# Graph layer and mixture of experts on one core: four more adds by GpSimd, column blocks loaded in halves, the first expert slot run tile by tile

## The chip, the cores and the metric

The kernel runs on one core of a Trainium2 chip. Its time is the device time in microseconds; where several executions are shown, the median counts, and lower is better.

## The reference

There are 2048 nodes with 256 features, 67,584 edges sorted by destination, and 8 experts of which each node takes the best two. Cut to what matters:

```python
    edge_index = jnp.stack([src, dst])
    x = x + _L0_gnn_ref(_layernorm(x, axis=-1), edge_weight, edge_index, node_vec1)
    x = x + _L0_ffn_ref(_layernorm(x, axis=-1)[None], L0_ffn_Wr, ...)[0]

def _L0_gnn_ref(x, values, indices, bias):
    gathered = values[:, None] * x[indices[1]]
    return jax.ops.segment_sum(gathered, indices[0], num_segments=2048) + bias

def _L0_ffn_ref(x, Wr, br, ln_g, ln_b, W1, b1, W2, b2):
    probs = jax.nn.softmax(xt @ Wr + br, axis=-1)
    top_p, top_idx = jax.lax.top_k(probs, 2)
    weights = top_p / top_p.sum(axis=-1, keepdims=True)
    xe = xn[None] * ln_g[:, None] + ln_b[:, None]
    h = jax.nn.gelu(jnp.einsum('end,edh->enh', xe, W1) + b1[:, None], approximate=False)
    y = jnp.einsum('enh,ehd->end', h, W2) + b2[:, None]
    # the two chosen experts' rows, weighted and summed
```

`xn` is the layer norm of `xt` once more. Hidden width is 1024.

## The kernel before

**First half: the graph layer.** The sum over edges is made into a matrix product. The 2048 columns (destinations) are cut into 16 *column blocks* `cb` of 128. For each block the kernel builds the dense block of the adjacency matrix (2048 rows by 128 columns) and multiplies it with the normalised features. The build runs in 32 steps `n`, two per block (`h = n % 2`). In a step:

- VectorE makes, for step n + 1, the one-hot operands `hl` (line 328), `eq` (335) and `hr` (343). Both `hl` and `hr` have two buffers.
- TensorE multiplies them for step n in 96 small matmuls (`make_cols`, line 367) into `pa` (three PSUM buffers), and ScalarE copies `pa` to `ar` (line 370; pool `rowsp`, three buffers).
- SP stores `ar` to a DRAM tile `ad` (line 371), which turns the layout around: step h = 0 writes rows 0 to 63 of the block, step h = 1 rows 64 to 127. After the second store SP loads the whole block back as `ac` (line 374), 1 MB. SP issues its transfers in program order, so the load stands in the queue until both stores have landed, and whatever is behind it stands too.
- `ac` tiles come from two pools: `cols_0` with three buffers (blocks 0 to 2, then 8 to 10) and `cols_1` with five (blocks 3 to 7, then 11 to 15). A buffer is free when the last product that reads it is done.

Column blocks are consumed in five groups (0-2, 3-6, 7-10, 11-13, 14-15). From n = 8 on each step also runs one *visit* (`dense`, line 383): the product of one group with two of the 16 row blocks, into a PSUM tile of two buffers. A group has eight visits: group 0 at n = 8 to 15, group 1 at n = 16 to 23, group 2 at n = 24 to 31, the rest after the loop. The result of a visit is added to `acc` one step later. For group 0 (`add_apart`) ScalarE copies it to SBUF tiles `st` (five buffers), adding the bias `node_vec1`, and GpSimd starts a transfer that adds `st` to `acc` (line 396). For later groups VectorE adds from PSUM (`add`, line 388).

The order on every engine here is the order of the program (`manual_schedule`). GpSimd also issues, in between, the gathers of edge windows (line 242) and runs (line 223). At n = 12 SP issues two fills of zeros (lines 588, 590).

**Second half: the experts.** After the graph layer the nodes are normalised, routed, and listed by expert. The work is cut into *slots*: 256 rows (two tiles of 128) that go to one expert. For a slot the rows are gathered by GpSimd, turned by TensorE and scaled by VectorE (`turn_rows`, lines 1027, 1030, `scale_rows`, line 1042), multiplied with W1 followed by GELU on ScalarE (`layer_1`, lines 1068, 1070), multiplied with W2 (`layer_2`, line 1082), weighted by VectorE (line 1085) and scattered with addition to DRAM (line 1090). The first three slots (`early`) are filled from the first ten row blocks alone, so that TensorE has expert work while the rest of the routing runs. In the first of them, `whole[0]`, six warming matmuls precede the turning, and two pieces of routing on TensorE (`list_batch_0` at c = 4, `sum_counts` at c = 7) are placed between the eight column tiles c of `layer_1`.

Of the kernel before, what the change touches and what calls it, by code (L numbers as in the profile page):

```python
# [10 lines left out]
F32 = mybir.dt.float32  # L11
# [3 lines left out]
AF = mybir.ActivationFunctionType  # L15
OP = mybir.AluOpType
# [6 lines left out]
P = 128  # L23
# [4 lines left out]
def kernel(  # L28
# [30 lines left out]
    nc = tc.nc  # L59
    N, D = x.shape  # L60
    NE, _, H = W1.shape
    E = src.shape[0]
    NB = N // P
    EJ = E // P
    KD = D // P
    KH = H // P
# [19 lines left out]
    NU = NF + NE  # L86
    DX = D + NE
    RW = D + 4
    AHEAD = 2
    EARLY = 3  # L90

# [261 lines left out]
    def make_cols(n, hl, hr):  # L353


        cb, h = n // 2, n % 2
        if h == 0:
            ads[cb] = dram.tile([P, NB, P], F32, name="ad", bufs=CB)
        ad_v = ads[cb].rearrange("(m j) b r -> (j b) m r", m=GB // QP)
        ar = rowsp.tile([P, GH // QP, P], F32, name="ar")  # L360
        for m0 in range(0, GH // QP, 4):
            pa = ps_a.tile([P, 4, P], F32, name="pa")
            for m in range(4):
                for i in range(3):
                    for j in range(QP):
                        g = (m0 + m) * QP + j
                        nc.tensor.matmul(pa[j * RK:(j + 1) * RK, m, :], hr[:, g, i, :],  # L367
                                         hl[:, g, :], start=(i == 0), stop=(i == 2),
                                         tile_position=(0, j * RK))
            nc.scalar.copy(ar[:, m0:m0 + 4, :], pa)  # L370
        nc.sync.dma_start(ad_v[:, h * GH // QP:(h + 1) * GH // QP, :], ar)
        if h == 1:
            acs[cb] = (cols_0 if cb in GROUPS[0] or 8 <= cb < 11 else cols_1).tile([P, NB, P], F32, name="ac")
            nc.sync.dma_start(acs[cb], ads[cb])

    def dense(blocks, b, between={}):

# [9 lines left out]
    def add(b, pa):  # L387
        nc.vector.tensor_add(acc[:, b:b + 2, :], acc[:, b:b + 2, :], pa[:, :, :DX])  # L388

    def add_apart(b, pa):  # L390
        st = stage.tile([P, 2, DX], F32, name="st")
        for i in range(2):
            nc.scalar.activation(st[:, i, :D], pa[:, i, :D], AF.Identity,
                                 bias=nv_c[:, b + i:b + i + 1], scale=1.0)
        nc.scalar.copy(st[:, :, D:], pa[:, :, D:DX])
        nc.gpsimd.dma_start(acc[:, b:b + 2, :], st, accum_op=OP.add)

    ads, acs = {}, {}
# [2 lines left out]
    with tc.manual_schedule(engines=ALL):  # L401
# [111 lines left out]
        for n in range(NH):  # L513
# [30 lines left out]
                b = {7: 0, 10: 4, 12: 8, 14: 12}[n]  # L544
                weigh_n(slice(b, b + 4))
            for p in late:
                (add_apart if n <= NB else add)(*p)
            late = []
            make_cols(n, *hots.pop(n))
            g, k = divmod(n - NB // 2, NB // 2)  # L550
# [161 lines left out]
    with tc.manual_schedule(engines=ALL - {ET.Pool}):  # L712
# [74 lines left out]
        def count(s):  # L787

            sel = s["sel"]
            more = route.tile([P, NE], F32, name=f"more{s['i']}", bufs=1)  # L790
            nc.vector.tensor_reduce(more, sel.rearrange("p b e -> p e b"), AX.X, OP.add)
            nc.vector.tensor_add(seen, seen, more)

        def sum_counts(s):

            sel, seen_b = s["sel"], s["seen"]
            s["pc"] = pc = counts[:, s["i"], :s["n"], :]
            nc.tensor.matmul(pc, before, sel, start=True, stop=False)
# [222 lines left out]
        def turn_rows(s, warm=0):  # L1021


            xs = sets[s.set][0]
            pt = ps_x.tile([P, KD, TS], F32, name="px")
            for i in range(warm):
                nc.tensor.matmul(pt[:, 0, :P], ident, ident, start=True, stop=True)
            for t in range(s.n):
                for k in range(KD):
                    nc.tensor.transpose(pt[:, k, t * P:(t + 1) * P],  # L1030
                                        xs[:, t, k * P:(k + 1) * P], ident)
            scale_rows(s, pt)
# [26 lines left out]
        def layer_1(s, between={}):  # L1059
            xs, w1, w2, ec, b2r = sets[s.set]  # L1060
            xeT = heads[s.head][0]
            hT = slotp.tile([P, KH, TS], F32, name="hT")
            for c in range(KH):
                if c in between:
                    between[c]()
                ph = ps_h.tile([P, TS], F32, name="ph")[:, :s.n * P]
                for k in range(KD):
                    nc.tensor.matmul(ph, w1[:, k, c * P:(c + 1) * P], xeT[:, k, :],  # L1068
                                     start=(k == 0), stop=(k == KD - 1))
                nc.scalar.activation(hT[:, c, :s.n * P], ph, AF.Gelu, bias=ec[:, c:c + 1],  # L1070
                                     scale=1.0)
            return hT

        def layer_2(s, hT, put, between={}):
            w2 = sets[s.set][2]
            xeT, wt, b2w = heads[s.head]
            for t in range(s.n):
                if t in between:
                    between[t]()
                py = ps_y.tile([P, D], F32, name="py")  # L1080
                for c in range(KH):
                    nc.tensor.matmul(py, hT[:, c, t * P:(t + 1) * P], w2[:, c, :],  # L1082
                                     start=(c == 0), stop=(c == KH - 1))
                ys = slotp.tile([P, D], F32, name="ys", bufs=4)
                nc.vector.scalar_tensor_tensor(ys, py, wt[:, t:t + 1], b2w[:, t, :], op0=OP.mult,  # L1085
                                               op1=OP.add)
                put(s, t, ys)
# [87 lines left out]
        ps_h = ctx.enter_context(tc.tile_pool(name="ps_h", bufs=3, space=PSUM))  # L1175
        ps_y = ctx.enter_context(tc.tile_pool(name="ps_y", bufs=2, space=PSUM))
        roots(last_b)
        turn_rows(whole[0], 6)
        enlist_rows(first_b)
        count(first_b)  # L1180
        take_seen(last_b)

# [7 lines left out]
        best(last_b, 0)  # L1190
        best(last_b, 1)
        select(last_b)
        hT = layer_1(whole[0], {4: list_batch_0, 7: lambda: sum_counts(last_b)})
        scale_recs(last_b, range(NB - NA))
        shares(last_b)
        nc.scalar.activation(warm, eps_sb, AF.Gelu)
# [91 lines left out]
```

## Time and profile before

| what | value |
|---|---|
| median of three runs | 491.8 us (488.56 to 492.25) |
| the profiled execution | 487.33 us |
| its span, first to last instruction | 485.6 us |
| mean granted TensorE clock | 0.989 |
| busy: TensorE, VectorE, ScalarE, GpSimd | 441.7, 268.2, 198.4, 173.3 us |
| loop over n ends on TensorE | about 189.4 us |
| first slot's layer 1 begins on TensorE | 231.43 us |

A row of the profile names the source line, the engine, the operation, and the tiles as out<-in. In a timeline a row begins with its start and its duration in us; what stands in square brackets is the idle time of the engine before it and what ended that. PE is TensorE, DVE VectorE, ACT ScalarE, POOL GpSimd, and SP the engine that issues most transfers; SPq rows are the issuing itself. An fp32 matmul shows as two records, so a product of four column blocks with two row blocks is x16.

### The profile page before, as it was taken

To read this page: it belongs to the slowest core of one execution; us is meant where nothing else is said; L and a number is where in the kernel's file an instruction comes from. 1 tells how busy PE (TensorE), PEld (TensorE's weight loads), DVE (VectorE), ACT (ScalarE), POOL (GpSimd) and SP (SyncE) were. 2 spreads that over 40 slices of the span, in tenths; PEclk is the share of its full clock that TensorE was granted. 3 is DMA by queue.
4 is the path that set the end of the run, shared out by engine and by line. 5 is a ranking of instruction groups with operands and counts; after the bars stand their busy time and mean duration, and the time that the engine had idled before them with its cause. 6 is when DMAs were issued, how large, how long until landed. Compare 5 with 4: busy or idle time off the path is not lost. (4 is left out here: it accounts for less than half of the span.)

```text
span 485.6 us, 12168 instructions
## 1 busy us (share of the span) xinstructions
PE 441.7 (91%) x5008; PEld 378.2 (78%) x5008; DVE 268.2 (55%) x556; ACT 198.4 (41%) x488; POOL 173.3 (36%) x141
## 2 busy tenths in 40 slices
PE   1587798889998999998999999999999999999995
PEld 0466677677886888887888888888888888879784
DVE  5999999999999974247772312334323212210011
ACT  2567669652423220066572233332334332224320
POOL 5560737654130000013724333564343444222123
PEclk9988899999999999999999999999999999999999
DMA  3777769988778776995438987799999676542341
GB/s 96 236 206 225 235 185 259 268 208 235 222 203 247 225 214 187 343 374 163 98 98 266 332 262 220 225 349 369 349 330 292 175 228 190 167 115 26 79 154 43
DMA packets 88372, 105.58 MB, mean 217 GB/s; under 512 B 9920, under 2 KB 77616, under 8 KB 86192
## 3 DMA queue, kind: packets, MB, share of 16 engines
q1 hardware_dynamic: 79072, 88.95, 57.7%
q0 software_dynamic: 9200, 15.67, 14.4%
q8 instruction: 44, 0.72, 0.6%
q14 instruction: 24, 0.20, 0.1%
q10 hardware_dynamic: 32, 0.04, 0.0%
HBM read 75.11 MB, written 29.47 MB: 215 GB/s over the span
## 5 line engine op out<-in xcount | busy, mean ns | idle before, releaser
L1068 PE MATMUL ph<-xeT,w 128*128 128x256 f32 (+1 forms) x576 | 122.7, 369 | 3.6 <-PEq L1242 1.2
L1082 PE MATMUL py<-w,hT 128*128 128x256 f32 x544 | 120.4, 379 | 0.0
L1070 ACT ACTIVATE hT<-ph,ec 128x256 f32<-128x256 f32 (+1 forms) x144 | 65.7, 460 | 128.8 <-PE ph L1068 74.2
L1068 PEld LDWEIGHTS ph<-xeT,w 128*128 128x128 f32 x576 | 103.7, 190 | 18.2 <-issue 2.9
L1082 PEld LDWEIGHTS py<-w,hT 128*128 128x128 f32 x544 | 102.2, 190 | 13.2
L1090 POOL DMA_INDIRECT y_d<-ys,to_i x30 | 48.0, 1598 | 115.0 <-DVE ys L1085 75.5
L383 PE MATMUL py<-xn_lo,ac 128*128 128x264 f32 x352 | 85.3, 394 | 4.1 <-DMA ac<-ad 3.6
L383 PEld LDWEIGHTS py<-xn_lo,ac 128*128 128x128 f32 x352 | 64.8, 190 | 17.2 <-DMA ac<-ad 4.5
L328 DVE TENSOR_TENSOR hl<-k,iota_b 128x4096 bf16<-128x4096 bf16 (+1 forms) x33 | 73.2, 2219 | 1.2 <-ACT k L289 1.0
L367 PE MATMUL pa<-hl,hr 128*32 128x128 bf16 x3072 | 54.9, 231 | 15.3 <-DVE hr L343 9.0
L367 PEld LDWEIGHTS <-hr 128*32 128x32 bf16 x3072 | 48.0, 103 | 25.3 <-issue 11.6
L1085 DVE SCALAR_TENSOR_TENSOR ys<-py,wt,b2w 128x256 f32<-128x256 f32 x34 | 16.3, 483 | 80.4 <-PE py L1082 77.2
L343 DVE TENSOR_TENSOR hr<-eq,w 128x3072 bf16<-128x3072 bf16 x32 | 56.2, 1758 | 1.9 <-DVE eq L335 0.5
L1042 DVE TENSOR_SCALAR xeT<-px,ec 128x256 f32<-128x256 f32 (+1 forms) x38 | 18.4, 525 | 67.0 <-PE px L1030 67.0
L370 ACT COPY ar<-pa 128x512 f32<-128x512 f32 x64 | 35.4, 592 | 39.0 <-PE pa L367 23.5
L995 POOL DMA_INDIRECT xs<-xr_d,to_i x32 | 33.5, 1045 | 15.0 <-DVE ys L1085 5.5
L242 POOL DMA_INDIRECT win_s<-in_src,at_i x8 | 15.9, 1987 | 60.7 <-DVE at_i L238 46.2
L383 PE MATMUL py<-xn_hi,ac 128*128 128x264 f32 x160 | 36.5, 388 | 0.3 <-PEq L613 0.3
L383 PEld LDWEIGHTS py<-xn_hi,ac 128*128 128x128 f32 x160 | 30.2, 190 | 5.7 <-PEq L613 0.7
L388 DVE TENSOR_TENSOR acc<-acc,py 128x528 f32<-128x528 f32 x29 | 20.3, 700 | 19.6 <-PE py L383 19.5
L1057 ACT ACTIVATE b2w<-b,wt 128x256 f32<-128x256 f32 x36 | 16.3, 499 | 25.7 <-DVE wt L1055 22.6
L335 DVE TENSOR_TENSOR eq<-k,iota_b 128x1024 bf16<-128x1024 bf16 x32 | 21.9, 683 | 0.0
(218 smaller groups left out, 331.5 us busy)
## 6 DMA issues: line engine op xcount, KB each, us to landing
w<-in_L_ffn_W SPq DMA_DIRECT2D x40, 1024.0 KB, 9.7
ad<-ar SPq DMA_DIRECT2D x32, 512.0 KB, 7.5
ac<-ad SPq DMA_DIRECT2D x16, 1024.0 KB, 6.0
b<-in_L_ffn_b SPq DMA_DIRECT2D x20, 128.0 KB, 8.6
acc<-st POOLq DMA_DIRECT2D x8, 264.0 KB
acc<-in_x SPq DMA_DIRECT2D x4, 512.0 KB, 4.5
out<-y_d SPq DMA_DIRECT2D x4, 512.0 KB, 5.0
xr_d<-rec SPq DMA_DIRECT2D x1, 1300.0 KB
```

The costliest lines, as they stand in the source:

```text
L328: nc.vector.tensor_tensor(hl.rearrange("p g (n t) -> p g n t", t=2)[:, m], two(k2[:, 0], g, P)[:, m], pair(P)[:, m], OP.is_equal)
L335: nc.vector.tensor_tensor(eq.rearrange("p g (n t) -> p g n t", t=2), two(k2[:, 1], g, RK), pair(RK), OP.is_equal)
L343: nc.vector.tensor_tensor(hr.rearrange("p g i (n t) -> p (g i) n t", t=2), eq[:, :, None, :].to_broadcast([P, GH, 3, RK]), w[:, :, None, : ...
L367: nc.tensor.matmul(pa[j * RK:(j + 1) * RK, m, :], hr[:, g, i, :], hl[:, g, :], start=(i == 0), stop=(i == 2), tile_position=(0, j * RK))
L370: nc.scalar.copy(ar[:, m0:m0 + 4, :], pa)
L383: nc.tensor.matmul(pa[:, i, :DX], acs[c][:, b + i, :], xn(c), start=(c == blocks[0]), stop=(c == blocks[-1]))
L388: nc.vector.tensor_add(acc[:, b:b + 2, :], acc[:, b:b + 2, :], pa[:, :, :DX])
L995: nc.gpsimd.indirect_dma_start(out=(sets[s.set][0] if into is None else into)[:, t, cols], out_offset=None, in_=(xr_d if rows is None else ...
L1068: nc.tensor.matmul(ph, w1[:, k, c * P:(c + 1) * P], xeT[:, k, :], start=(k == 0), stop=(k == KD - 1))
L1070: nc.scalar.activation(hT[:, c, :s.n * P], ph, AF.Gelu, bias=ec[:, c:c + 1], scale=1.0)
L1082: nc.tensor.matmul(py, hT[:, c, t * P:(t + 1) * P], w2[:, c, :], start=(c == 0), stop=(c == KH - 1))
L1090: st = nc.gpsimd.indirect_dma_start(out=y_d[:, :], out_offset=bass.IndirectOffsetOnAxis(ap=tos[s.to][:, t:t + 1], axis=0), in_=ys, in_offs ...
```

## The change

Three edits are made together.

1. For the second group, the visits whose results are added at n = 17 to 20 also go through `st` and GpSimd's adding transfer; the copy to `st` is then one plain ScalarE copy without bias. The other four visits stay with VectorE.
2. The load of a column block is split into two halves of 64 partitions. Half 0 reads only rows that the first store wrote. In step h = 1 it is issued ahead of the second store, except for blocks 11 and 15, where it follows that store. Half 1 always comes last.
3. In the first slot, turning, scaling and layer 1 go one tile of 128 rows at a time. The second tile is turned inside the first tile's layer (ahead of c = 4); column tiles go in pairs that share a PSUM tile; the two pieces of routing move to the second tile's layer, at c = 2 and c = 6.

```diff
+    WAIT = 11, 15
...
+        def get_half(i):
+            rows = slice(i * P // 2, (i + 1) * P // 2)
+            nc.sync.dma_start(acs[cb][rows], ads[cb][rows])
+
+        if h == 1:
+            acs[cb] = (cols_0 if cb in GROUPS[0] or 8 <= cb < 11 else cols_1).tile([P, NB, P], F32, name="ac")
+            if cb not in WAIT:
+                get_half(0)
         nc.sync.dma_start(ad_v[:, h * GH // QP:(h + 1) * GH // QP, :], ar)
         if h == 1:
-            acs[cb] = (cols_0 if cb in GROUPS[0] or 8 <= cb < 11 else cols_1).tile([P, NB, P], F32, name="ac")
-            nc.sync.dma_start(acs[cb], ads[cb])
+            if cb in WAIT:
+                get_half(0)
+            get_half(1)
...
-    def add_apart(b, pa):
+    def add_apart(b, pa, first):
         st = stage.tile([P, 2, DX], F32, name="st")
-        for i in range(2):
-            nc.scalar.activation(st[:, i, :D], pa[:, i, :D], AF.Identity,
-                                 bias=nv_c[:, b + i:b + i + 1], scale=1.0)
-        nc.scalar.copy(st[:, :, D:], pa[:, :, D:DX])
+        if first:
+            for i in range(2):
+                nc.scalar.activation(st[:, i, :D], pa[:, i, :D], AF.Identity,
+                                     bias=nv_c[:, b + i:b + i + 1], scale=1.0)
+            nc.scalar.copy(st[:, :, D:], pa[:, :, D:DX])
+        else:
+            nc.scalar.copy(st, pa[:, :, :DX])
         nc.gpsimd.dma_start(acc[:, b:b + 2, :], st, accum_op=OP.add)
...
-                (add_apart if n <= NB else add)(*p)
+                if n <= NB + 4:
+                    add_apart(*p, n <= NB)
+                else:
+                    add(*p)
...
+        def turn_tile(s, pt, t, warm=0):
...
+            rows = slice(t * P, (t + 1) * P)
+            for i in range(warm):
+                nc.tensor.matmul(pt[:, 0, :P], ident, ident, start=True, stop=True)
+            for k in range(KD):
+                nc.tensor.transpose(pt[:, k, rows], xs[:, t, k * P:(k + 1) * P], ident)
+            for k in range(KD):
+                nc.vector.tensor_scalar(xeT[:, k, rows], pt[:, k, rows], ec[:, KH + k:KH + k + 1],
+                                        ec[:, KH + KD + k:KH + KD + k + 1],
+                                        op0=OP.mult, op1=OP.add)
+
+        def layer_1_tile(s, hT, t, between={}):
...
+            for c in range(0, KH, 2):
+                if c in between:
+                    between[c]()
+                ph = ps_h.tile([P, TS], F32, name="ph").rearrange("p (i r) -> p i r", r=P)
+                for i in range(2):
+                    for k in range(KD):
+                        nc.tensor.matmul(ph[:, i, :], w1[:, k, (c + i) * P:(c + i + 1) * P],
+                                         xeT[:, k, rows], start=(k == 0), stop=(k == KD - 1))
+                for i in range(2):
+                    nc.scalar.activation(hT[:, c + i, rows], ph[:, i, :], AF.Gelu,
+                                         bias=ec[:, c + i:c + i + 1], scale=1.0)
...
-        turn_rows(whole[0], 6)
+        pt = ps_x.tile([P, KD, TS], F32, name="px")
+        hT = slotp.tile([P, KH, TS], F32, name="hT")
+        turn_tile(whole[0], pt, 0, 6)
         enlist_rows(first_b)
+        layer_1_tile(whole[0], hT, 0, {4: lambda: turn_tile(whole[0], pt, 1)})
...
-        hT = layer_1(whole[0], {4: list_batch_0, 7: lambda: sum_counts(last_b)})
+        layer_1_tile(whole[0], hT, 1, {2: list_batch_0, 6: lambda: sum_counts(last_b)})
```

More of the change, by code (lines that the diff above doesn't have):

```diff
@@ L1072, in layer_1 @@
             return hT
+        def turn_tile(s, pt, t, warm=0):
+            xs, w1, w2, ec, b2r = sets[s.set]
+            xeT = heads[s.head][0]
+            rows = slice(t * P, (t + 1) * P)
[8 more added lines that the diff above has]
+        def layer_1_tile(s, hT, t, between={}):
+            xs, w1, w2, ec, b2r = sets[s.set]
+            xeT = heads[s.head][0]
+            rows = slice(t * P, (t + 1) * P)
+            for c in range(0, KH, 2):
[9 more added lines that the diff above has]
+                                         bias=ec[:, c + i:c + i + 1], scale=1.0)
         def layer_2(s, hT, put, between={}):
```

## The prediction

> **What bounds the kernel now.** I read the page first. TensorE is busy for 91% of the span, and the chain that ended last covers only the last 15 us, so the question is where TensorE waits, and for whom. I then read TensorE's timeline. From 231.43 us to the end it has almost no gap, and from 189.4 to 228 it has almost none either. Time that it wins or loses earlier reaches the end one for one. These are its waits in the second half of the loop over n:
>
> ```profile
> 100.65 1.60 PE L383 MATMUL py<-xn_lo,ac 128*128 128x264 f32 x6
> 103.89 2.49 PE L383 MATMUL py<-xn_lo,ac 128*128 128x264 f32 x10 [1.64 <-DMA ac<-ad]
> ...
> 113.72 0.85 PE L367 MATMUL pa<-hl,hr 128*32 128x128 bf16 x48 [1.01 <-ACT ar L370]
> ...
> 149.68 2.49 PE L383 MATMUL py<-xn_lo,ac 128*128 128x264 f32 x10 [1.98 <-DMA ac<-ad]
> ...
> 157.64 1.52 PE L367 MATMUL pa<-hl,hr 128*32 128x128 bf16 x96
> ...
> 162.85 1.52 PE L367 MATMUL pa<-hl,hr 128*32 128x128 bf16 x96
> ```
>
> Lines two and four are the first visits of the second and third group (n = 16 and 24), stopped at their last column block (6 and 10) until its load lands. Line three waits for a copy into `ar`, which waited for a store `ad<-ar`. The last two give a step without waits: 5.21 us, about 0.6 more where keys are turned, so about 10.7 per column block of two steps. VectorE is busy almost throughout but is not what TensorE waits for. Its `hr` for n = 24 starts at 141.11, takes 1.76 and is ready at 142.87; TensorE begins that step at 144.64. From n = 17 to 30 VectorE is 1.8 to 4.4 us ahead.
>
> Behind all three waits stands SP's queue. The list of what SP waits for, then its timeline:
>
> ```profile
> SPq L374 <- DMA ad<-ar: 103.9, 16, 13.6
> ...
> SPq L371 <- ACT ar L370: 40.7, 14, 11.2
> ```
> ```profile
> 84.05 0.33 SPq L374 DMA_DIRECT2D ac<-ad  x1
> ...
> 98.47 0.33 SPq L374 DMA_DIRECT2D ac<-ad  x1
> 98.85 2.24 SPq L371 DMA_DIRECT2D ad<-ar  x2
> 114.73 0.33 SPq L374 DMA_DIRECT2D ac<-ad  x1
> 115.11 1.82 SPq L371 DMA_DIRECT2D ad<-ar  x2
> 124.35 0.33 SPq L374 DMA_DIRECT2D ac<-ad  x1
> 124.73 1.12 SPq L371 DMA_DIRECT2D ad<-ar  x2
> 133.35 0.33 SPq L374 DMA_DIRECT2D ac<-ad  x1
> ```
>
> The reader is to see the rhythm. SP stands at each load for the landing of the block's stores, and when it is released the next block's two stores are already waiting and leave at once. So here SP and the transfers set the pace. From load to load undisturbed it takes 9.0 to 9.6 us, less than TensorE's 10.7. From 72.49 to 114.73, however, it takes 11.6, 14.4 and 16.3, and in that stretch the first group's eight transfers by GpSimd run:
>
> ```profile
> 99.18 3.69 POOL L396 DMA_DIRECT2D acc<-st  x4
> ```
>
> 42.2 us instead of three times 9.3 leaves 14.3 us for eight such transfers, two zero fills and gathers. Four transfers (1.06 MB) were in one interval of 16.3, which is 7.0 over; they are about three quarters of GpSimd's bytes there, so I charge about **1.3 us each**.
>
> **The change, part by part.**
>
> *Adds by GpSimd.* VectorE loses four `acc<-acc,py` at n = 17 to 20, 4 x 0.70 = 2.8 us. TensorE lags VectorE there, so this is worth 0 unless TensorE's waits go away. ScalarE gains four copies of 128x528 (the nearest row, 128x512, takes 0.59): 2.4 us in a stretch where it is busy a third of the time, 0. They stand ahead of the `ar` copies and need only the visit that TensorE has just ended. GpSimd issues four more transfers, queued behind the three window gathers of n = 17 (until 114.8); the next gathers come at 131.7, so nothing waits on its queue. What they cost is transfer time: 4 x 1.3 = **5.2 us** just where SP is the pace. Low bound 0 (they fall where the transfer engines idle, as while SP waits), high bound 4 x 1.75 = 7.0 (all of the excess above).
>
> *Half loads.* The count of bytes stays. What changes is the order on SP: half 0 now stands ahead of the second store and waits there for the landing of the first store. Behind it on SP are that store, and with three `ar` buffers ScalarE's copy three steps on, then TensorE's `pa`. One round per block (wait for two stores, load) becomes two (wait for one store, half load). Cost of a round: this answer is the time from issue to landing of a whole load (source line 374).
>
> ```profile
> DMA to landing us min/median/max: 5.9/6.0/6.1
> ```
>
> A load and two stores behind it take 9.0 to 9.3 from load to load, so a store behind a load adds 1.5 to 1.65. A store alone, issued at 25.14, releases the load at 28.88: 3.7, so about 1.4 to 2.2 is latency and the load's own transfer is 3.8 to 4.6. A new round is latency 1.4 to 2.2, half a load 2.3 to 1.9, a store 1.5: **5.2 to 5.6 us**, two to a block 10.4 to 11.2. I take 10.6, nearest to the low end because the longer latency is seen once, on an idle queue. That is **1.3 us more per block** than 9.3, and all the spare time that SP has against TensorE's 10.7. On the other side the last wait gets shorter: half 1 lands 1.9 to 2.3 us sooner after its issue than a whole load.
>
> Here the Trainium skill (DMA: Bandwidth & Descriptors, "Rules for kernel authors") speaks against the change: transfers on disjoint partition halves share the same engines, so one over all partitions is advised. Its fit (same page, "Anatomy of one DMA", given for GpSimd's path) is 2.0 us plus bytes over 436 GB/s. By it a new round with 1 MB is 4.4 us, 8.8 a block, and would hide under TensorE's 10.7; the measured 9.0 for 2 MB (6.8 by the fit) says that its rate is too high here, so I keep 10.6.
>
> Sum to block 6. SP still has idle time early on (the 40.7 us of waits for `ar`). Walking the first stores with 5.3 a round, half 1 of block 3 leaves at about 65.3, where the load now leaves at 62.61: 2.7 late. Three further blocks at 1.3 make 3.9; half 1 lands 2.2 sooner. Together +4.4, so TensorE's wait at n = 16 grows from 1.64 to about 6. Sum to block 10: four more blocks, 5.2, and the added transfers, 5.2, of which TensorE's own delay of 4.4 covers part. So does the time that SP now waits for `ar` from 114.7 on (three blocks of 9.6 instead of 9.0, 1.8). 5.2 + 5.2 - 4.4 - 1.8 = 4.2, and 0.4 for short waits on `ar` before: 4.6. VectorE's 2.8 us stay hidden, as TensorE lags more. After n = 24, blocks 11 and 15 keep the old order and the loop ends with SP again close behind. The loop thus ends about **9.0 us later**.
>
> *First slot tile by tile.* The start of this slot now, and the pace of a 128-column layer in the later half slots:
>
> ```profile
> 228.68 0.38 PE L1030 MATMUL px<-ident,xs 128*128 128x128 f32 x2
> 230.35 0.44 PE L1030 MATMUL px<-ident,xs 128*128 128x128 f32 x2 [1.29 <-DMA xs<-x_d,to_i]
> 231.43 3.74 PE L1068 MATMUL ph<-xeT,w 128*128 128x256 f32 x16 [0.64 <-DVE xeT L1042]
> ```
> ```profile
> 444.37 3.73 PE L1068 MATMUL ph<-xeT,w 128*128 128x128 f32 x32
> ```
>
> Tile 0's rows are there at 228.68. Two transposes (0.38) and two scalings of 128 columns (0.41 each, overlapping: about 0.8) let the layer begin at about 229.95 instead of 231.43: 1.5 won. 64 matmuls of half width take 2 x 3.73 = 7.46 against 7.07 (0.4 lost); tile 1's transposes now stand inside (0.4 lost). Tile 1's rows land before they are wanted (230.3 against 231.8), and VectorE has its chain of `select` ready at about 237.4 as now, just before the counts at 238. ScalarE needs 3.44 for eight half-width GELUs, under TensorE's 3.73. Net **-0.7 us** (+0.5 if the counts wait for VectorE, -1.5 at best).
>
> Sum: +9.0 - 0.7 = +8.3. The profiled execution took 487.33 (span 485.6) and would take 495.6; the median shown is 491.8, 4.5 above it, so I add the same: **500 us**.
>
> **Rivals.** *SP gets slower but TensorE does not see it* (chance 0.25): a round nearer 5.0 and the added transfers filling idle stretches, so the halves' later issue and sooner landing cancel. For it: the transfer share is only 0.80 between 115 and 190. Against: SP already paces at 115. Change between -5 and +5; with waits as now, 491.8 - 0.7 = 491.
> *The waits vanish* (0.14): half 1 lands early enough at n = 16 and 24 and `ar` never waits; 1.64 + 1.01 + 1.98 = 4.6, with 0.7: 486.5. It decides where a round stays under about 4.7 us, so that SP reaches block 6 no later than now and half 1's 2 us come out as gain; then VectorE's 2.8 us would be needed, since its lead falls to 1.8. This is the other side.
> *A whole-block wait* (0.04): if the second store had to wait for half 0's landing (2 to 4 us more, fourteen blocks), 30 us and more, beyond 520. That now both stores of a block leave within 1.1 us (124.73) speaks against such coarse tracking.
>
> **How the numbers follow.** The slower queue has 0.57: from +5 (transfers at their low bound, rounds 5.2) to +19 (all high). Slower by over 1% (4.9 us, about what a measurement of this kernel can tell from no change) takes this and the whole-block wait: 0.61. Within 1%: 0.25. Faster: 0.14. The likeliest case alone is 497 to 511. The range runs from 486, which takes in the second rival and the near half of the third, to 511, leaving out the top of the likeliest and the whole-block wait.
>
> **What would show it.** Right: from block 3 on SP standing at half 0 with the second store issued right after; issues of half 1 10 us and more apart and late at blocks 6 and 10; TensorE waiting for `ac` 5 us or so at n = 16 and more than 2 at n = 24. Wrong: waits for `ac` below 1 us and the loop ending before 189. For the slot: its first `ph` 1.3 us after the first transposes, with no wait between tiles. A store that lands in 3 us behind a half load would overturn the round, and with it the sign.

## The result and the profile after

The changed kernel takes **522.2 us** (median of 7 runs, 518.42 to 530.54) where the kernel before takes 491.8 (median of 7, 488.56 to 494.44): +30.4 us between the medians. Some executions of every kernel fall into a slower state; ratios are of the others alone, here 1.0597, interval 1.0547 to 1.0646. The forecast was 500 with a range to 511. The direction was right, the size was not.

The profiled execution took 530.54 us (span 528.5), 8.4 above its median, at a mean granted clock of 0.942, while that of before lay 4.5 below its median; so only 30 of the 43 us between the two profiles stand in the medians. The waits for column blocks and for the first rows that follow come back, about as long, in two further profiles of the changed kernel (e0 and e12); the wait for `ar` does not (0.48 and 0.18 us there).

First the same views as before. Rows from the list of groups: busy us and mean ns of one, then the idle time ahead of the group and what ended most of it. The first fence is of before, the second of after.

```profile
L383 PE MATMUL py<-xn_lo,ac 128*128 128x264 f32 x352 | 85.3, 394 | 4.1 <-DMA ac<-ad 3.6
...
L367 PE MATMUL pa<-hl,hr 128*32 128x128 bf16 x3072 | 54.9, 231 | 15.3 <-DVE hr L343 9.0
```
```profile
L393 PE MATMUL py<-xn_lo,ac 128*128 128x264 f32 x352 | 91.9, 415 | 24.0 <-DMA ac<-ad 24.0
...
L368 PE MATMUL pa<-hl,hr 128*32 128x128 bf16 x3072 | 58.7, 239 | 16.0 <-DVE hr L344 9.5
```

For the dense products both figures have grown: 20 us more waiting for column blocks, and 6.6 us more for the same matmuls. TensorE's timeline says where; the first fence is again of before (its other rows stand in the prediction):

```profile
189.43 15.29 PE L383 MATMUL py<-xn_hi,ac 128*128 128x264 f32 x68
```
```profile
65.53 3.86 PE L393 MATMUL py<-xn_lo,ac 128*128 128x264 f32 x8 [3.22 <-DMA ac<-ad]
...
110.85 0.85 PE L368 MATMUL pa<-hl,hr 128*32 128x128 bf16 x48 [2.66 <-ACT ar L371]
...
126.96 4.74 PE L393 MATMUL py<-xn_lo,ac 128*128 128x264 f32 x10 [13.72 <-DMA ac<-ad]
...
180.62 4.25 PE L393 MATMUL py<-xn_lo,ac 128*128 128x264 f32 x10 [7.04 <-DMA ac<-ad]
...
221.63 15.29 PE L393 MATMUL py<-xn_hi,ac 128*128 128x264 f32 x68
...
269.78 0.69 PE L1099 MATMUL px<-ident,xs 128*128 128x128 f32 x2 [8.74 <-DMA xs<-x_d,to_i]
```

In the second fence, rows one, three and four are the first visits of the three groups, at n = 8, 16 and 24, each stopped at its last block (2, 6, 10). Row two is a wait for a copy into `ar`. Then come the end of the loop, 221.63 where it was 189.43 (+32.2); and the first slot, whose rows are now late (they were there at 228.68, so +41.1). SP's queue, from the list of what it waits for, and its timeline where no adding transfer of GpSimd runs:

```profile
SPq L374 <- DMA ad<-ar: 162.7, 32, 9.8
...
SPq L380 <- ACT ar L371: 16.8, 14, 11.2
```
```profile
157.83 0.45 SPq L374 DMA_DIRECT2D ac<-ad  x1
158.33 0.58 SPq L380 DMA_DIRECT2D ad<-ar  x1
163.92 0.45 SPq L374 DMA_DIRECT2D ac<-ad  x1
164.42 0.58 SPq L380 DMA_DIRECT2D ad<-ar  x1
169.91 0.45 SPq L374 DMA_DIRECT2D ac<-ad  x1
170.41 0.58 SPq L380 DMA_DIRECT2D ad<-ar  x1
175.83 0.45 SPq L374 DMA_DIRECT2D ac<-ad  x1
```

SP now stands 32 times, 162.7 us in all (before: 16 times, 103.9), and in this stretch one half load and one store go out together, never two stores. One round takes 6.0 us (157.83, 163.92, 169.91, 175.83), a block two, 11.9 to 12.1. TensorE needs 10.7. Undisturbed, SP was the faster one of the two by 1.4 us per block before; now it is the slower one by 1.2. Where GpSimd's adding transfers run, rounds take up to 11.8 us.

Then there is the granted clock. These rows are stretches of the span: the length, the busy time of PE, PEld (loading weights), DVE, ACT and POOL with the number of instructions, and the last three figures are the granted clock, the DMA share and the GB/s. The first fence is of after, the second of before.

```profile
113.00:127.00 14.00, 0.28 (x3) 0.07 (x1) 3.70 (x5) 2.15 (x7) 3.86 (x4) 0.61 0.88 207
...
172.00:181.00 9.00, 1.96 (x11) 1.45 (x8) 5.93 (x8) 1.07 (x2) 0.00 (x0) 0.80 0.81 211
...
270.00:283.00 13.00, 12.50 (x106) 12.07 (x106) 7.68 (x31) 4.82 (x16) 9.86 (x10) 0.75 0.20 53
```
```profile
113.00:127.00 14.00, 13.29 (x281) 11.12 (x281) 13.29 (x15) 6.03 (x13) 1.79 (x1) 1.00 0.69 188
```

After each long wait TensorE goes on at a lower clock: the ten dense matmuls behind the wait of 13.72 us take 4.74 us, those behind the waits of before (1.6 and 2.0 us) 2.49. Behind the 2.66 us for `ar` the 48 small matmuls take 0.85, as in the kernel before. The Trainium skill (TensorE: Matmul & The Clock Gate, Part 1) tells why: a gate halves the clock after an idle window, and it takes some us of work to come back. The trace agrees with the half (4.74 to 2.49); the length of the window is not measured here. The forecast charged nothing for it; how much of it reaches the end is worked out below.

### The profile page after: what moved, and what is told of

Same layout as the page of the kernel before. It is cut to its first block, busy times and chain, and to the rows that moved or that the text cites. A ratio compares the mean times of both kernels' runs of the same rounds, so it can differ in the third digit from the quotient of the medians.

```text
span 528.5 us, 12287 instructions
## 1 busy us (share of the span) xinstructions
PE 457.4 (87%) x5040; PEld 392.5 (74%) x5040; DVE 267.0 (51%) x554; ACT 202.0 (38%) x500; POOL 166.4 (31%) x145
## 5 line engine op out<-in xcount | busy, mean ns | idle before, releaser
L1084 PE MATMUL ph<-xeT,w 128*128 128x256 f32 (+1 forms) x544 | 115.2, 368 | 3.0 <-PEq L1294 1.0
L393 PE MATMUL py<-xn_lo,ac 128*128 128x264 f32 x352 | 91.9, 415 | 24.0 <-DMA ac<-ad 24.0
L1084 PEld LDWEIGHTS ph<-xeT,w 128*128 128x128 f32 x544 | 98.0, 190 | 16.7 <-issue 3.0
L1086 ACT ACTIVATE hT<-ph,ec 128x256 f32<-128x256 f32 (+1 forms) x136 | 62.0, 461 | 123.8 <-PE ph L1084 69.7
L393 PEld LDWEIGHTS py<-xn_lo,ac 128*128 128x128 f32 x352 | 68.8, 202 | 39.1 <-issue 25.3
L329 DVE TENSOR_TENSOR hl<-k,iota_b 128x4096 bf16<-128x4096 bf16 (+1 forms) x33 | 73.3, 2223 | 26.8 <-PE pa L368 25.7
L368 PE MATMUL pa<-hl,hr 128*32 128x128 bf16 x3072 | 58.7, 239 | 16.0 <-DVE hr L344 9.5
L368 PEld LDWEIGHTS <-hr 128*32 128x32 bf16 x3072 | 51.4, 107 | 26.5 <-issue 13.0
L371 ACT COPY ar<-pa 128x512 f32<-128x512 f32 x64 | 35.5, 590 | 53.9 <-DMA ad<-ar 30.4
L398 DVE TENSOR_TENSOR acc<-acc,py 128x528 f32<-128x528 f32 x25 | 17.4, 701 | 26.2 <-PE py L393 26.2
L243 POOL DMA_INDIRECT win_s<-in_src,at_i x8 | 12.2, 1520 | 48.4 <-DVE at_i L239 30.7
L409 POOL DMA_DIRECT2D acc<-st x12 | 10.8, 1003 | 43.6 <-ACT st L408 25.9
```

The costliest lines, as they stand in the source:

```text
L329: nc.vector.tensor_tensor(hl.rearrange("p g (n t) -> p g n t", t=2)[:, m], two(k2[:, 0], g, P)[:, m], pair(P)[:, m], OP.is_equal)
L393: nc.tensor.matmul(pa[:, i, :DX], acs[c][:, b + i, :], xn(c), start=(c == blocks[0]), stop=(c == blocks[-1]))
```

## The experiments

Theory A: the half loads are the loss, because SP stands twice per block and the second store stays behind the first standing. Rivals: B, the added GpSimd transfers; C, the start of the first slot; D to H, as each run names them. The runs fell on several chips, so each is read against the kernel before on its own chip. In the table the us are medians of all executions. The medians of the kernel before were 497.53 for e0 to e3, 489.77 for e5, e6, e7 and e9, 496.95 for e8, e10, e11 and e12, 490.82 for e4 and e14 to e16.

| run | what it is | us | times before, interval |
|---|---|---|---|
| e0 | the changed kernel, one execution | 538.5 | none |
| e12 | the changed kernel | 540.7 | 1.0845 (1.0739 to 1.0951) |
| e1 | half loads alone | 531.7 | 1.0693 (1.0609 to 1.0776) |
| e2 | adds by GpSimd alone | 501.5 | 1.0152 (1.0052 to 1.0252) |
| e3 | first slot by tiles alone | 500.8 | 1.0060 (1.0028 to 1.0093) |
| e4 | the changed kernel without half loads | 495.2 | 1.0118 (1.0028 to 1.0208) |
| e5 | halves, both behind the second store | 491.4 | 0.9994 (0.9967 to 1.0021) |
| e6 | half 0 issued by ScalarE | 500.9 | 1.0232 (1.0186 to 1.0278) |
| e7 | whole load one step later | 499.2 | 1.0160 (1.0121 to 1.0199) |
| e9 | half 0 first in every second block | 511.5 | 1.0425 (1.0349 to 1.0501) |
| e10 | half loads, five `ar` buffers | 531.2 | 1.0668 (1.0563 to 1.0773) |
| e15 | whole loads, 64 bytes where half 0 stood | 516.3 | 1.0537 (1.0384 to 1.0690) |
| e8 | changed, weights behind the row stores | 535.4 | 1.0754 (1.0651 to 1.0857) |
| e14 | changed, weights behind the gathers | 518.4 | 1.0567 (1.0470 to 1.0663) |
| e11 | before, zero fills at n = 4 | 497.7 | 0.9988 (0.9939 to 1.0037) |
| e16 | e5 with the fills at n = 4 | 489.5 | 0.9954 (0.9923 to 0.9986) |

### Which of the three edits

**e0, e12: the changed kernel again.**

> The changed kernel once more, for a second profile. The first one has three large waits of TensorE for column blocks (3.22, 13.72 and 7.04 us) and one of 8.74 us for the first slot's rows behind the loop. If the queue of SP is the cause, all four are there again, at about the same length, because the order of SP's queue does not change from run to run; a time of 518 to 526 us. If the 8.74 us are an accident of that one execution, it is under 3 us here and the time is nearer to 518.

> The changed kernel unchanged, timed beside the next three. Expected as first measured: about 1.06 times before, with waits for ac near 3, 14 and 7 us at blocks 2, 6 and 10 and 8 to 9 us for the first slot's rows.

The waits for `ac` were 2.96, 14.87 and 8.11 us in e0 and 4.57, 13.61 and 8.27 in e12, those for the first rows 8.50 and 9.02. The ratio on this chip is higher, 1.0845 instead of 1.0597. In both profiles TensorE shows some pauses of 0.3 to 1 us within the first slot that wait for nothing the profile shows; whether they make the difference between the chips was not tried.

**e1, e2, e3: one edit alone.** Each is the diff of the change, cut to one edit, on the kernel before.

> The half loads alone, the other two edits left out. Theory A (two waits of SP per column block instead of one, 5.9 us each by the changed profile, so 11.9 per block against 9.3): nearly all of the loss is here, 512 to 522 us, with waits for the sixth and tenth block of several us. Theory B (the four added transfers by GpSimd are what loads the DMA engines): 495 to 503. Theory C (the loss is in the first slot's start): about 492.

> The four more adds by GpSimd alone. Theory A: the queue of SP has about 1.4 us to spare per block here, so that 4 transfers of 1.3 us cost at most 2 to 5 us at block 10: 492 to 497. Theory B: 505 or more. Theory C: 492.

> The first slot tile by tile alone. Theories A and B: the layer starts about 1.5 us sooner and is 0.8 us longer, so 0.7 us is won, 491 us, and TensorE's wait for tile 1's rows is gone. Theory C: 500 or more, with a long wait for rows ahead of the first slot.

e1 has most of the loss, 34 us where e0 on the same chip has 41 in its one execution (its 531.7 lies above the 512 to 522 expected, on a chip where before itself takes 5.7 us longer). The waits are at the same places:

```profile
127.82 4.30 PE L393 MATMUL py<-xn_lo,ac 128*128 128x264 f32 x10 [8.06 <-DMA ac<-ad]
...
180.56 4.74 PE L393 MATMUL py<-xn_lo,ac 128*128 128x264 f32 x10 [5.85 <-DMA ac<-ad]
...
270.32 0.69 PE L1040 MATMUL px<-ident,xs 128*128 128x128 f32 x2 [8.26 <-DMA xs<-x_d,to_i]
```

e2 costs 1.5% (2.6 to 12.5 us), between what A and B expected. In its profile three loads of SP from 116.00 to 149.25 take 33.25 us where before took 28.86 (114.73 to 143.59), 4.4 more, but TensorE does not feel it there: it is 6.2 us later than in the profile of before at block 6 already (110.12), ahead of the added transfers, and 5.4 later at block 10 (155.09). e4, further down, shows their cost on TensorE. e3 costs 0.6%, where a gain of 0.7 us was forecast; its profile has four pauses of TensorE within the slot, 4.1 us together, that are put down to instruction issue. It is of a rather long execution (506.02 us), and the cause of the 0.6% stays open.

**e4: the changed kernel without half loads.**

```diff
-        def get_half(i):
...
+        nc.sync.dma_start(ad_v[:, h * GH // QP:(h + 1) * GH // QP, :], ar)
         if h == 1:
...
-            if cb not in WAIT:
-                get_half(0)
...
+            nc.sync.dma_start(acs[cb], ads[cb])
```

> The changed kernel with whole column-block loads put back as before; the four adds by GpSimd and the first slot tile by tile stay. Theory A (the half loads are the loss, the other two edits cost 1.5% and 0.6% when alone): 1.015 to 1.025 times before. If the edits feed on each other, more than 1.03.

1.0118, about the sum of e2 and e3 within their intervals. Here the added transfers show on TensorE:

```profile
104.40 2.49 PE L383 MATMUL py<-xn_lo,ac 128*128 128x264 f32 x10 [1.53 <-DMA ac<-ad]
...
154.15 3.88 PE L383 MATMUL py<-xn_lo,ac 128*128 128x264 f32 x10 [2.98 <-DMA ac<-ad]
...
195.28 15.29 PE L383 MATMUL py<-xn_hi,ac 128*128 128x264 f32 x68
```

Against the profile of before it is 0.5 us late at block 6, 4.5 at block 10 and 5.9 at the end of the loop, so 5.3 came in the stretch where they run and behind it. The slot itself can be seen without a wait ahead of it:

```profile
234.53 0.38 PE L1089 MATMUL px<-ident,xs 128*128 128x128 f32 x2
235.41 2.15 PE L1107 MATMUL ph<-xeT,w 128*128 128x128 f32 x16 [0.51 <-DVE xeT L1091]
...
244.58 0.60 PE L1036 MATMUL px<-ident,xs 128*128 128x128 f32 x4
```

From the first transposes to the end of the layer it is 10.05 us, before 11.39 (228.68 to 240.07): the edit does what it says, and gains 1.3 us. In the changed kernel the same stretch took 12.84 (269.78 to 282.62), at clocks of about 0.75: the same 16 matmuls take 3.78 instead of 2.15. So behind the wait of 8.74 us the layer took 2.8 us more.

### Order, bytes or buffers

**e5: halves, but both behind the second store.** The edit is shown against e1, as are those of e9 and e6.

```diff
-    WAIT = 11, 15
+    WAIT = tuple(range(16))
```

> The kernel before with half loads alone, and for every block both halves stand behind the second store. The bytes, the number of transfers and the halves stay as in the half loads alone (531.7 us beside 497.5); only the place of half 0 in SP's queue goes back. Theory A (SP meets a wait twice per block, and each costs a round of 5.9 us): one wait per block is left, load to load about 9.3 to 10 us, TensorE's waits for ac as in before (1 to 2 us at n = 16 and 24); time within 1% of before, at most +5 us. Rival D (a load cut into halves of 64 partitions is itself dear, because its packets take 0.55 us instead of 0.47 and it starts 1.24 us after its issue instead of 0.97): the two halves land at 7 us or more after the issue of the first instead of 6.0, a block takes about 11 us, and half or more of the loss, +15 us, stays.

0.9994: with the same bytes and the same number of half loads the loss is gone, so D is out. TensorE waits nowhere over 0.8 us for a block. SP's timeline shows the rhythm of before, with two stores leaving together:

```profile
114.25 2.00 SPq L374 DMA_DIRECT2D ac<-ad  x2
116.34 1.17 SPq L380 DMA_DIRECT2D ad<-ar  x2
123.81 2.05 SPq L374 DMA_DIRECT2D ac<-ad  x2
125.92 1.34 SPq L380 DMA_DIRECT2D ad<-ar  x2
132.76 2.28 SPq L374 DMA_DIRECT2D ac<-ad  x2
```

That is 9.0 to 9.6 us per block. SP still meets two waits per block here, but they end 1.5 to 2.7 us apart, since both stores are in flight. So Theory A has to be put more sharply: what costs is not a second wait, it is that the second store isn't in flight while SP waits for the first.

**e15: only the standing.**

```diff
+        if h == 1 and cb not in (11, 15):
+            probe = small.tile([1, 16], F32, name="probe")
+            nc.sync.dma_start(probe, ads[cb][0:1, 0, 0:16])
         nc.sync.dma_start(ad_v[:, h * GH // QP:(h + 1) * GH // QP, :], ar)
```

> The kernel before, whole loads, and where half 0 stood (ahead of the second store, all blocks but 11 and 15) a transfer of 64 bytes that reads the first store's rows; it adds no output. Only the standing is left. If the standing alone is the cause: per block, first store behind a load lands at about 7.5 us after that load's issue, second store 3.7 later, load to load 11.2 to 11.5 us against TensorE's 10.7; a loss of 70 to 90% of that of the half loads, +22 to +30 us, waits for ac at blocks 6 and 10 of 4 us and more. If the half load's own transfer in the round is what costs: under a third, at most +10 us.

```profile
139.69 0.34 SPq L377 DMA_DIRECT2D ac<-ad  x1
140.09 0.45 SPq L374 DMA_DIRECT2D ad<-ar  x1
147.09 0.25 SPq L373 DMA_DIRECT2D probe<-ad  x1
147.39 0.38 SPq L374 DMA_DIRECT2D ad<-ar  x1
150.64 0.34 SPq L377 DMA_DIRECT2D ac<-ad  x1
```

64 bytes ahead of the second store cost 5.4% (18.8 to 33.9 us); the half loads alone cost 6.9% (e1). Load to load is 11.45, 10.95 and 11.5 us from 128.24 on: 7.4 until the first store, queued behind the load, has landed, then 3.2 to 3.6 for the second one by itself. The waits at block 6 (4.85) and for `ar` (4.32 and 6.51) are there, at block 10 it is only 0.99, where 4 or more were expected. So the standing alone brings most of the loss. Whether the half load's own transfer adds the rest is not shown: the two intervals (3.8 to 6.9% and 6.1 to 7.8%) overlap, and the runs fell on two chips.

**e10: more buffers.**

```diff
-    rowsp = pool("rowsp", 3)
+    rowsp = pool("rowsp", 5)
```

> The half loads alone, with five buffers for ar instead of three. Theory A (SP's pace through its two waits per block is what counts; the buffers only say where TensorE feels it): TensorE's waits for ar (9.3 us together in the half loads alone) go, and come back as longer waits for ac at blocks 6 and 10, since SP passes no sooner; 1.06 to 1.075 times before, as the half loads alone. Rival H (the stores held up behind half 0 cost only because ar runs out of buffers): the waits for ar go and nothing comes in their place; 9 us less, 1.05 or below.

1.0668: 5.6 to 7.7% of loss stay, so H is out as the whole cause. The waits for `ar` (9.3 us in e1) are gone, but those at blocks 6 and 10 did not grow, as A had it: they are 7.07 and 3.98, with one of 2.13 at block 2. The product behind block 10 starts 5.2 us sooner than in e1 (175.40 to 180.56), so SP does pass somewhat sooner; at the first slot it is 4.1 (266.22 to 270.32) and at the end of the span 2.0. How much the buffers are worth in time is not shown, since e1 ran on another chip.

**e9: half the dose.**

```diff
-    WAIT = 11, 15
+    WAIT = tuple(range(1, 16, 2))
```

> The half loads alone, with half 0 ahead of the second store only in the even blocks; odd blocks have both halves behind it. Half the dose. Theory A with a threshold (SP's pace against TensorE's 10.7 us per block): even blocks 11.9, odd about 9.5, mean 10.7, just TensorE's pace; so waits for ac stay near those of before plus what SP loses early: 0 to +8 us. Rival F (each half load ahead of a store costs TensorE its share directly, no slack): half of the 34 us, +15 to +19 us.

+21.7 us, more than either expected.

```profile
118.36 4.66 PE L393 MATMUL py<-xn_lo,ac 128*128 128x264 f32 x10 [12.43 <-DMA ac<-ad]
```
```profile
102.54 0.45 SPq L374 DMA_DIRECT2D ac<-ad  x1
103.03 1.01 SPq L380 DMA_DIRECT2D ad<-ar  x1
113.39 0.45 SPq L374 DMA_DIRECT2D ac<-ad  x1
```

Block 6 is one of the even blocks, and its round (102.54 to 113.39) fell into GpSimd's adding transfers and took 10.9 us instead of 6. Half 1 of block 6 leaves 14.9 us later than the load did before (98.47), and the loop ends 14.9 us later (204.37). At block 10 nothing waits any more: from 113.39 to the half 1 of block 10 at 156.59 it is 10.8 us per block, and that is enough. So the threshold holds in the calm part, and does not up to block 6, where SP already was the pace: there what SP loses is passed on in full.

**e6: half 0 from another queue.**

```diff
             if cb not in WAIT:
-                get_half(0)
+                nc.scalar.dma_start(acs[cb][:P // 2], ads[cb][:P // 2])
```

> The half loads alone, but half 0 is issued by ScalarE, behind its copies into ar of the same step; half 1 and the stores stay on SP. Same halves, same order of readiness, but SP no longer stands at half 0. Theory A (the loss is SP standing in its queue a second time): SP issues half 1 every 9 to 10.7 us, TensorE's waits for ac fall to 0 to 2 us, and since half 1 lands about 1.2 us sooner after its issue than a whole load the time is at or a little below before: -3 to +3 us. Rival E (the transfers themselves are in each other's way: half 0 beside the second store makes that store land late): SP's wait at half 1 grows above 3.7 us, half 1 goes out later than the whole load in before, waits at blocks 6 and 10 stay above 3 us, +10 us or more.

+11.1 us, as much as rival E expected, but not in its way: TensorE waits for no block, so neither half was too late. ScalarE stands in SP's place:

```profile
90.45 0.45 ACTq L379 DMA_DIRECT2D ac<-ad  x1
90.95 0.40 ACT L276 ACTIVATE cl<-win_d,col 128x128 f32<-128x128 int32 x1 [9.07 <-DMA ad<-ar]
```
```profile
91.73 0.47 PE L310 MATMUL pk<-ident,f 128*128 128x128 f32 x1 [5.07 <-DVE f L281]
```

Behind half 0 on ScalarE is `cl`, for which VectorE waits, for which TensorE waits. Here ScalarE, which issues the transfer in its own order of work, stands for it just as SP does. Whether rival E has a part is not shown: SP's longest wait for a store is 9.6 us, but it was 13.6 in the kernel before.

**e7: the whole load a step later.** `get_cols` allocates `acs` and issues the whole load, which goes from its old place.

```diff
...
+        if h == 0 and cb and cb - 1 not in WAIT:
+            get_cols(cb - 1)
+        if h == 1 and cb in WAIT:
+            get_cols(cb)
```

> The kernel before with whole loads, each issued one step later: behind the first store of the next block (block 15 at once, as before). The opposite of the half loads: SP should meet no wait at a load at all, since the block's second store went out a step (5.2 us) earlier and lands in 3.7 to 6. Theory A (what costs is SP's standing at a load, with the next stores behind it): SP's waits for ad<-ar fall from 104 us to under 40, the waits of TensorE for ac at blocks 6 and 10 and for ar (4.6 us together) mostly go, load of block 6 out at about 94 to 96 us instead of 98.5; 2 to 5 us below before. Rival (transfer time is the pace, not the standing): loads land as late as now or later by the step they were put off, waits at blocks 6 and 10 stay or grow by 1 to 3 us; 0 to +6 us.

```profile
SPq L380 <- DMA ad<-ar: 34.9, 7, 8.8
```
```profile
114.01 4.77 PE L389 MATMUL py<-xn_lo,ac 128*128 128x264 f32 x10 [5.48 <-DMA ac<-ad]
```

My expectation missed: SP's standing fell from 103.9 us to 34.9, as it should, and the kernel got 1.6% slower (5.9 to 9.7 us). The load of block 6 left at 106.14 instead of 98.47, since it was put off by a step, and the load of block 5 ahead of it waited for a store that took 12.7 us to land in GpSimd's stretch (82.89 to 95.61). The sum of SP's waits is no measure of the loss; the time at which the load leaves and lands is.

### Behind the loop

In the changed kernel SP leaves the loop with the load of block 15 at 229.00 (before 192.63), 7.4 us after TensorE has (before 3.2). The weights of three slots, 6 MB, come next on its queue, and then the stores of the rows that the first slot's gathers read.

**e8 and e14: those weights moved.** In both, the weights of the second and third slot are taken out of the first place; e8 puts them behind the stores of `x1_d`, e14 behind the gathers (the edit shown is e14's). They are 4 MB, not the 3 of the expectations.

```diff
-            get_weights(whole[u], W1[u:u + 1], cols_d[u:u + 1], W2[u:u + 1], b2[u:u + 1])
+            if u == 0:
+                get_weights(whole[u], W1[u:u + 1], cols_d[u:u + 1], W2[u:u + 1], b2[u:u + 1])
...
             get_rows(whole[u], rows=sh_d, n=NA * P, cols=slice(D, RW))
+        for u in range(1, EARLY):
+            get_weights(whole[u], W1[u:u + 1], cols_d[u:u + 1], W2[u:u + 1], b2[u:u + 1])
```

> The changed kernel, with the weights of the second and third expert slot loaded behind the stores of the first slots' rows (x1_d) instead of ahead of them; the loop over n is untouched. Theory A, last step (SP leaves the loop late, so 3 MB of weights stand ahead of the rows that the first slot waits for): TensorE's wait for xs, 8.5 to 8.7 us, falls to 1.5 us or less, and the time is 6 to 8 us below the changed kernel. Rival G (the rows are late for another reason: adds, squares or routing on VectorE come late by themselves): the wait stays above 6 us, the time within 2 us of the changed kernel. If the second slot then waits for its weights instead, the gain is smaller and the wait shows there.

> The changed kernel, with the weights of the second and third slot loaded behind the gathers of the first slots' rows. Theory A, last step (3 MB of weights are ahead of the rows in the queues, either ahead of their stores or beside their gathers): TensorE waits 2 us or less for xs, 7 us below the changed kernel in the profile, unless the second slot now waits for its weights. Rival G (something else is late): 4 us of waiting or more stay.

e8: the first gather, which in e12 waited 18.20 us for the row stores, no longer does, but lands 9 us after its issue, beside the moved weights:

```profile
260.66 1.06 POOL L1011 DMA_INDIRECT xs<-x_d,to_i  x1 [8.90 <-DVE acc L398]
```
```profile
269.99 0.69 PE L1099 MATMUL px<-ident,xs 128*128 128x128 f32 x2 [6.17 <-DMA xs<-x_d,to_i]
```

The time is 5.3 us less than e12 beside it, and the wait of 6.17 decides nothing between A and G. e14: the gather leaves at 258.00, and the transposes follow the warming matmuls without a wait:

```profile
261.01 0.38 PE L1099 MATMUL px<-ident,xs 128*128 128x128 f32 x2
261.89 2.15 PE L1117 MATMUL ph<-xeT,w 128*128 128x128 f32 x16 [0.51 <-DVE xeT L1101]
```

So the rows are late because of the weights in the queues, and G is out. The changed kernel wasn't timed on e14's chip, so the gain is read from the profiles only: the loops end alike (221.76 and 221.63), the layer begins 9.1 us sooner, and the span is 7.3 us shorter (521.2 to 528.5). Some is lost again later, 2.2 of it in a wait for gathered rows at 302.89.

### Is there something faster?

e11 moves the two fills of zeros, which stand ahead of block 6's load, to n = 4 (the two `dma_start` under `if n == 12` go under `if n == 4`); e16 does so in e5.

> The kernel before with the two fills of zeros (512 KB together) issued by SP at n = 4 instead of n = 12, where they stand ahead of the load of block 6. It asks how much of the slow stretch before block 6 is theirs, and whether a version faster than both kernels lies there. Theory A (SP's queue and the transfers are the pace from about 75 to 115 us): the load of block 6 leaves 3 to 4 us sooner, the waits at block 6 and for ar (2.6 us) go, 1 to 4 us below before. Rival (the fills lie beside SP's standing anyway): no difference, within 1 us.

> The kernel before with both halves behind the second store for every block (0.9994 times before) and the zero fills at n = 4 (0.9988). TensorE waits for no load in either kernel's first 140 us or so. If its waits for ac were worth their time: 0.990 to 0.997 times before. If the time lost at those waits is only handed to the next wait on its way (VectorE's one-hot operands, instruction issue): 0.997 to 1.003.

e11: no difference. The wait at block 6 is gone, one of 3.39 us at block 10 came, and its profile has pauses by issue as well. e16: 0.9954, interval 0.9923 to 0.9986, half a per cent below before and the shortest of all, with no wait of TensorE for `ac` over 0.8 us. It beats both kernels, by less than 1% the one before. Where the gain lies is not shown: in its profile the loop ends at 192.38, later than the 189.43 of the kernel before, with a pause of 4.15 us put down to issue.

## Why the prediction was wrong

**What held.** The place and the order of events: half 0 stands, the store goes out 0.5 us behind it, issues of half 1 are more than 10 us apart, TensorE waits at n = 16 and at n = 24. The charge for the added transfers (5.2; in time 2.6 to 12.5 in e2, on TensorE 5.3 in e4). VectorE's saved work, at nothing: its `hl` now waits 26.8 us for TensorE (1.2 of waiting before).

**The step that failed is the price of a round.** It was put as "latency 1.4 to 2.2, half a load 2.3 to 1.9, a store 1.5: 5.2 to 5.6", taken as 5.3. Measured: 6.0. Between 150 and 180 us the half load took 4.7 to 4.9 us from issue to landing, so with 3.7 to 4.1 its share was sized too small (1.4 + 2.3 to 2.2 + 1.9); the store landed 1.1 to 1.5 after it, about as said. A load of 1 MB takes 6.0, one of 512 KB 4.8: half the bytes saved 1.2 us, not the 1.9 to 2.3 that went into the sum. A straight line through these two gives an estimate of 1.2 for the transfer of 512 KB and 3.6 for what doesn't depend on the bytes, while the sum had 1.4 to 2.2. The Trainium skill (DMA: Bandwidth & Descriptors, "Anatomy of one DMA") names, for GpSimd's path, a fixed part of some 2.0 us, most of it the completion; for these loads of SP, with stores queued behind them, the line gives more. The 0.7 us of a round is small, but it is paid twice per block, and the block goes from 10.6, just under TensorE's 10.7, to 11.9, above it. The range of the sum (10.4 to 11.2) lay across that threshold; I took a value 0.1 us below it and so let SP keep up.

**The walk to block 3 failed with it.** "2.7 late" at block 3, 2.7 + 3.9 at block 6. SP's issues of the load (before) and of half 1 (after):

| block | before | after | late |
|---|---|---|---|
| 3 | 62.61 | 73.59 | 11.0 |
| 6 | 98.47 | 121.96 | 23.5 |
| 10 | 143.59 | 175.83 | 32.2 |
| 15 | 192.63 | 229.00 | 36.4 |

I let the early part hide most of it, in the 40.7 us that SP waited for `ar` (now 16.8). But from the second half of block 1 rounds took 5.9 to 7.2 us there too. Blocks 4 to 6 added 12.5, where three times 2.6 is 7.8: the rest is rounds in GpSimd's stretch, up to 11.8 (e9 shows one of 10.9). So at block 6 TensorE was 23.1 us late (126.96 to 103.89) where the sum had 4.4, and this is ahead of the added transfers. Of these 18.7 us, as an estimate, 13 rounds from half 0 of block 0 on, each 0.7 dearer, make 9; 1.8 is half 1, which landed only 0.4 sooner after its issue than the whole load and not 2.2. The other 8 are rounds that took still longer than 6.0, beside transfers of GpSimd, the fills and TensorE's own early waits; these were not taken apart. So the wait at block 6 was 13.7 and not 6, and two waits that the forecast didn't have, 3.2 at block 2 and 5.0 for `ar`, precede it.

**The end of the loop**, forecast +9.0, was +32.2 in the profile. TensorE spent 20 us more in waiting for blocks, 3 for `ar`, and 10.4 on the same matmuls at a lower clock (dense 6.6, `pa` 54.9 to 58.7): together 33. This says what TensorE did, not what each part would save. Half 1 of block 10 left 32.2 late, and SP had waited for `ar` hardly at all (16.8 us, 11.2 of them in one wait ahead of its first store). The product that needs it starts 30.9 late, and from there to the end of the loop TensorE took 41.01 us, before 39.75. So SP's lateness is the loop's, and of the 10.4 us only about 1.3 came on top: the others lie ahead of a wait whose end SP sets.

**Behind the loop I had taken the delay as constant.** It grew by 8.9 (32.2 to 41.1), since SP was later still than TensorE and weights stood ahead of the rows (e14). In e5, e6 and e7, which leave the loop at most 12 us later than before, the wait for rows stays at 1.1 to 1.8.

**The first slot**: -0.7 was the sum; from the first transposes to the end of the layer the edit gives -1.3 at full clock (e4), +1.5 behind a wait (the changed kernel). Alone it measured +0.6%, unexplained. The three pieces, 32.2, 8.9 and 1.5, make 42.6 of the 42.9 us between the spans.

**The rivals.** "The waits vanish" and "TensorE does not see it" needed rounds of 4.7 and 5.0; both are out. The whole-block wait (beyond 520) comes near in its number, but not by its mechanism: the second store did not wait for half 0 to land. It went out 0.5 us behind half 0; it had been kept back before that, by half 0's own wait.

## What to carry to other kernels

An early start of half a transfer is paid by whatever stands behind it on the issuing queue. Before putting a transfer that waits ahead of one that is ready, ask what would be in flight meanwhile, and price the round with a measured time from issue to landing, not with bytes. Where one pace lies just under another, treat the sum as a threshold: give the chance of crossing it, and follow the delay to the end, into the queue behind the loop. Charge the lower clock after a long wait only where no later wait would swallow it.

## What was not expected of the hardware

- Halving a load of 1 MB (to 64 partitions of 8 KB) shortened it from 6.0 to 4.8 us only, with stores queued behind it in both kernels.
- One transfer of 64 bytes per block, in the wrong place of an in-order queue, cost about 26 us in all (e15).
- Behind a wait of 8.7 us the next 13 us of TensorE ran at a clock of 0.75, and a layer took 12.84 us instead of 10.05 (e4).
- Between chips the changed kernel's ratio differs (1.0597 and 1.0845, intervals apart; the cause was not tried), while the kernel before differs by up to 1.6% (489.8 to 497.5 us).
